# First token tile's gate product moved into the output banks, ahead of the second tile's dt product and running sums

## The chip, the core and the metric

The kernel runs on one core of one Trainium2 chip. The metric is device time in microseconds of one execution of the program. Timed runs of the kernel before gave 942.22 to 943.0, median 942.59.

## The reference

One layer on 256 tokens of width 512, all in fp32: a cross-attention to 4096 context rows, a Mamba-2 block, and a mixture of 32 experts, each added to the residual x. The change lies in the Mamba block, which with its projections and its scan is:

```python
zxbcdt = einsum("bld,ed->ble", u, W_in)          # u: layernorm of x
z, xBC, dt = split(zxbcdt)                       # 1024, 1280, 16 columns
xBC = silu(causal_conv1d(xBC, conv_w, conv_b))   # 4 taps, per channel
dt = softplus(dt + dt_bias); dA = dt * -exp(A_log)
A_cs = cumsum(dA)                                # within a chunk of 128 tokens
Lmat = tril(exp(A_cs[l] - A_cs[s]))
Y = C B^T * Lmat @ (x dt)  +  C @ state * exp(A_cs)  +  x D
y = rmsnorm(Y * silu(z)) * norm_weight
out = y @ W_out
```

## The kernel before, in words

The 256 tokens are two tiles of 128; each tile is one chunk of the scan, and only tile 1 receives a carried state. The whole layer is one program. Attention over the context fills the first 720 us; tile 0's share of the Mamba block up to its decays is run beside the last attention steps. Then come the output projection of attention for tile 1, the rest of the Mamba block, the routing, and the experts.

**Who sets the order.** The Python text calls small closures. A scheduler then gives every engine one fixed order, from the order of the text, the dependencies, the tile buffers and its own estimate of durations; so an instruction can stand earlier or later than its line. `tc.issue_after(x)` keeps what is issued under it behind instruction x in that order. On the chip each engine works through its own list and waits on semaphores.

**PSUM.** There are eight banks. Six are in a ring that `bank(name)` hands out in turn (pools `ps_mm`, `ps_sc`, `ps_tp`); the two others are `ps_o`, tag "o", in which `within(t)` makes a tile's output, `ps_yd`.

The steps of the Mamba block that matter here, with their names and the lines of the kernel before:

- `product()` of tile t: `turn_xn` transposes the layernorm's result on TensorE into a bank (`lnT`, L227) and copies it to `xT` in two halves, one on VectorE and one on ScalarE (L231). Then `project` (L237) makes the dt product `ps_dt`: four matmuls of 16 columns. VectorE adds the bias (L984) and ScalarE takes an exponential (L987).
- `series()`: some fifteen VectorE instructions on 128x16 values, softplus by a series, which end in `dA` (L1000).
- `sums()`: the running sums `ps_cs` (L1005), a matmul of `dA` with a triangle of ones, copied to `acs` (L1008).
- `decays(t)`: its first step, `spread_sums` (`lm[0]`), makes the sums transposed (`ps_csT`, L1023), copies them (L1024), writes them to DRAM by a DMA from ScalarE's queue (L1025), and reads them back from GpSimd's queue, broadcast to all partitions, into `lm` (L1026) and, for tile 1, into `e1` (L1030). Its four pieces subtract `acs` on VectorE (L1034, 16 instructions) and take the exponential on ScalarE (L1038); the last also takes that of `e1` (L1040).
- `channels(t)`: ten pieces, one for every 128 channels of xBC. Four matmuls (`ps_xbc`, L237), two ScalarE instructions (L1054, L1055), then three taps of the convolution, on VectorE (L1063), or for the channel tiles 3 and 7 on ScalarE and GpSimd (L1060, L1061). `active()` is one Silu over all ten (L1066), called as `silu[t]()`.
- `gates(t)`: for each half j of 512 columns of z, 16 matmuls of 128 columns (`ps_z`, L237) with the weights `w_z[j]`, and a Silu into `zs` (L1078).
- `assemble(t)`: `y` from `ps_yd` (L1153), times the gate (L1154), its square (L1155), times the norm's weight (L1156), and the sums of the squares (L1158).
- `tokens_back(t)`: eight transposes of the activated channels (`xtT`, L1088) and a product with dt (L1090).
- `mixing(t)`: `ps_g` (L1098) and its product with the decays, on VectorE and GpSimd (L1102).
- `carried(t)`, `within(t)`, `mamba_out(t)`: `ps_off` (L1136), `ps_yd` (L1110), and the output projection `ps_out` (L1163).
- `hold(...)`: gives buffers that are no longer needed to the experts' weights, and starts the loads on SyncE's queue (L1406); the first of them wait for the start of tile 1's decays.

The list `order` is the channel tiles 8, 9, 0, 1 ... 7: B and C first.

Of the kernel before, what the change touches and what calls it, by code (L numbers as in the profile page):

```python
# [11 lines left out]
FP = mybir.dt.float32  # L12
U32 = mybir.dt.uint32
I32 = mybir.dt.int32
AF = mybir.ActivationFunctionType
# [4 lines left out]
P = 128  # L20
# [9 lines left out]
REP = NH // NKV  # L30
# [10 lines left out]
SH = 16  # L41
# [3 lines left out]
CONV = 4  # L45
# [39 lines left out]
def perceiver_layer(ctx: ExitStack, tc: tile.TileContext, a: dict, out: bass.AP):  # L85
    nc = tc.nc
    V, S, G, TE = nc.vector, nc.scalar, nc.gpsimd, nc.tensor
# [62 lines left out]
    def layer(ctx, bounded):  # L150
# [10 lines left out]
        xT = keep.tile([P, KD, L], FP, name="xT")  # L161
# [62 lines left out]
        def turn_xn(t, tp, halves=False):  # L224

            for k in range(KD):
                TE.transpose(tp[:, k * P:(k + 1) * P], xn[:, t, k * P:(k + 1) * P], ident)  # L227

            for copy, ks in (((V.tensor_copy, slice(0, KD // 2)), (S.copy, slice(KD // 2, KD))) if halves else
                             ((V.tensor_copy, slice(0, KD)),)):  # L230
                turned = copy(xT[:, ks, t * P:(t + 1) * P], tp.rearrange("p (k n) -> p k n", k=KD)[:, ks])  # L231
            return turned

        def project(ps, lhs, rhs_of):

            for k in range(KD):
                last = TE.matmul(ps, lhs(k), rhs_of(k), start=(k == 0), stop=(k == KD - 1))  # L237
            return last

        conv_w, conv_b, norm_w, d_col = carve(by_channel, (XCT, CONV), (XCT,), (DIT,), (DIT,))  # L240
# [420 lines left out]
        q = [[lambda j=j, t=t: q_of(j, t) for t in range(NT)] for j in range(4)]  # L661
# [262 lines left out]
        ps_o = pool("ps_oT", 2, space=PSUM) if bounded else None  # L924
        m = {}
        banks = ring([(ps_mm, "mm")])

        def bank(name):
            p, tag = banks()
            return p.tile([P, 512], FP, tag=tag, name=name)  # L930
# [30 lines left out]
        tok = lambda t: slice(t * P, (t + 1) * P)  # L961
# [13 lines left out]
        def steps_of(t):  # L975


            vdt, nab, u, z, z2, ser, dt, dA, acs = (m[n, t] for n in ("vdt", "nab", "u", "z", "z2", "ser", "dt", "dA", "acs"))

            def product():  # L980
                turn_xn(t, bank("lnT"), halves=True)
                ps = bank("ps_dt")
                project(ps[:, 0:SH], lambda k: xT[:, k, tok(t)], lambda k: m["w_bcd"][:, k, 256:272])
                V.tensor_tensor(vdt, ps[:, 0:SH], dt_bias, ALU.add)  # L984
                V.tensor_scalar(nab, vdt, -1.0, None, ALU.mult)
                V.tensor_tensor(nab, nab, vdt, ALU.min)
                S.activation(u, nab, AF.Exp)  # L987

            def series():
                V.tensor_scalar(z, u, 2.0, None, ALU.add)  # L990
                V.reciprocal(z, z)
                V.tensor_tensor(z, z, u, ALU.mult)
                V.tensor_tensor(z2, z, z, ALU.mult)
                V.tensor_scalar(ser, z2, 1.0 / 15.0, None, ALU.mult)
                for d in (13, 11, 9, 7, 5, 3):
                    V.scalar_tensor_tensor(ser, ser, 1.0 / d, z2, ALU.add, ALU.mult)
                V.scalar_tensor_tensor(ser, ser, 1.0, z, ALU.add, ALU.mult)
                V.tensor_scalar(vdt, vdt, 0.0, None, ALU.max)
                V.scalar_tensor_tensor(dt, ser, 2.0, vdt, ALU.mult, ALU.add)
                V.scalar_tensor_tensor(dA, dt, -1.0, m["ea", 0], ALU.mult, ALU.mult)  # L1000

            def sums():

                ps = bank("ps_cs")
                TE.matmul(ps[:, 0:SH], upper, dA, start=True, stop=True)  # L1005
                if t == 0:
                    TE.matmul(ps[:, SH:2 * SH], ones, dA, start=True, stop=True)
                V.tensor_copy(acs, ps[:, 0:SH])  # L1008
                if t == 0:
                    V.tensor_tensor(m["decay", 0], ps[:, SH:2 * SH], acs, ALU.subtract)  # L1010
                    S.activation(m["decay", 0], m["decay", 0], AF.Exp)
            return product, series, sums

        decay_begun = []

        def decays(t):


            lm, acs = m["lm"], m["acs", t]

            def spread_sums():
                ps = bank("ps_csT")[0:SH, 0:P]
                TE.matmul(ps, m["dA", t], upper, start=True, stop=True)  # L1023
                S.copy(m["csT", t], ps)  # L1024
                S.dma_start(sums_d[t], m["csT", t])  # L1025
                G.dma_start(lm, sums_d[t].partition_broadcast(P))  # L1026
                if t > 0:
                    pairs = sums_d[t].rearrange("(c e) l -> e c l", e=2)
                    for i in range(2):
                        G.dma_start(m["e1"][lanes(i)], pairs[i].partition_broadcast(SP))  # L1030

            def piece(q):
                for hh in range(q * 4, q * 4 + 4):
                    begun = V.tensor_scalar(lm[:, hh, :], lm[:, hh, :], acs[:, hh:hh + 1], 0.0, ALU.subtract, ALU.min)  # L1034
                    if hh == 0:
                        decay_begun.append(begun)
                with tc.issue_after(gated[-1]) if gated else nullcontext():
                    S.activation(lm[:, q * 4:q * 4 + 4, :], lm[:, q * 4:q * 4 + 4, :], AF.Exp)  # L1038
                    if t > 0 and q == 3:
                        S.activation(m["e1"], m["e1"], AF.Exp)  # L1040
            return [spread_sums] + [lambda q=q: piece(q) for q in range(4)]

        def channels(t):


            xc, xraw = m["xc", t], m["xraw"]

            def piece(ct):
                w, c0 = ((w_x[ct // 4], ct % 4 * P) if ct < 8 else (m["w_bcd"], (ct - 8) * P))
                ps = bank("ps_xbc")[:, 0:P]  # L1050
                project(ps, lambda k: w[:, k, c0:c0 + P], lambda k: xT[:, k, tok(t)])
                xb = xraw[:, ct, :]
                y = xc[:, ct, :]
                S.copy(xb[:, CONV - 1:], ps)  # L1054
                S.activation(y, ps, AF.Identity, bias=conv_b[:, ct:ct + 1], scale=conv_w[:, ct, CONV - 1:CONV])  # L1055
                for j in range(CONV - 1):
                    w = conv_w[:, ct, j:j + 1]
                    if ct % 4 == 3:
                        tap = small.tile([P, P], FP, tag="tap", name="tap", bufs=2)
                        S.activation(tap, xb[:, j:j + P], AF.Copy, scale=w)  # L1060
                        G.tensor_tensor(y, y, tap, ALU.add)  # L1061
                    else:
                        V.scalar_tensor_tensor(y, xb[:, j:j + P], w, y, ALU.mult, ALU.add)  # L1063

            def active():
                S.activation(xc, xc, AF.Silu)  # L1066
                if t + 1 < NT:
                    G.tensor_copy(xraw[:, :, 0:CONV - 1], xraw[:, :, P:P + CONV - 1])
            return [lambda ct=ct: piece(ct) for ct in range(XCT)], active

        gated = []

        def gates(t):
            def piece(j):
                ps = bank("ps_z")
                for i in range(4):
                    project(ps[:, tok(i)], lambda k: w_z[j][:, k, tok(i)], lambda k: xT[:, k, tok(t)])
                gated.append(S.activation(m["zs"][:, t, j * 512:(j + 1) * 512], ps, AF.Silu).ins)  # L1078
            return [lambda j=j: piece(j) for j in range(2)]

        def tokens_back(t):

# [345 lines left out]
        run = lambda fs: [f() for f in fs]  # L1428
        order = [XCT - 2, XCT - 1] + list(range(XCT - 2))
# [18 lines left out]
        else:  # L1448
            general_attention()
            ps_o = pool("ps_oT", 2, space=PSUM)  # L1450
# [5 lines left out]
        product, series, sums = steps_of(1)  # L1456
        chans, silu = zip(*(channels(t) for t in range(NT)))
# [8 lines left out]
        w_z = [wpiece(a["W_inT"][:, c0:c0 + 512], f"w_in{c0}") for c0 in (0, 512)]  # L1466
# [7 lines left out]
        run(within(0))  # L1474
        state()
        routing_memory()
        product()
        series()
        lm = decays(1)
        run(chans[1][c] for c in order[0:3])  # L1480
        sums()
        lm[0]()
        run(chans[1][c] for c in order[3:])
        run(gates(0))
        run(lm[1:])

        hold(*w_x, lacc[:, 0], behind=decay_begun[-1])
# [1 line left out]
        silu[1]()  # L1489
        run(tokens_back(1))  # L1490
        mixing(1)()
        run(gates(1))
        hold(*w_z)
        run(carried(1))
        run(within(1))
# [19 lines left out]
        product, gate0, turn0 = shared_hidden(0)  # L1515
# [9 lines left out]
        product, gate1, turn1 = shared_hidden(1)  # L1525
# [184 lines left out]
        with ExitStack() as rctx:  # L1710
# [42 lines left out]
            copied = main.turn(0)  # L1753
# [103 lines left out]
    with tc.If(flag == 1) as arms:  # L1857
        with ExitStack() as lctx:
            layer(lctx, True)
# [51 lines left out]
```

## Time and profile before

| what | value |
|---|---|
| median of 3 runs | 942.59 us (942.22 to 943.0) |
| the profiled execution's own time | 946.23 us |
| its span, first to last instruction | 944.3 us |
| mean granted TensorE clock | 0.997 |
| PE busy | 924.2 us, 98% |
| weight loads on PE | 504.9 us, 53% |
| VectorE, ScalarE, GpSimd busy | 577.4, 370.0, 427.8 us |
| chain that ended last | PE 96%, VectorE 2% |
| all gate products, ps_z, in that chain | 1% of the span |

Times in the profile count from the span's start. PE is TensorE's matmuls, PEld its weight loads, DVE VectorE, ACT ScalarE, POOL GpSimd, SP SyncE. L12 is line 12 of the kernel. An fp32 matmul leaves two records. A line of the timeline gives the start, the duration, engine, line and operation, what it writes and reads, and in brackets the idle time before it with the instruction that ended it. The chain that ended last is followed back from the last instruction, at each step to what released it. PEclk is the clock that TensorE was granted, 1.00 at full speed.

### The profile page before, as it was taken

The numbers are of one execution on the slowest core, as the hardware profiler recorded it, in microseconds if no ns is written. First come the engines' busy times: TensorE is split into PE (matmuls) and PEld (weight loads), VectorE is DVE, ScalarE is ACT, GpSimd is POOL, SyncE is SP. The second block draws the span as 40 slices with busy tenths as digits, with TensorE's granted clock in tenths as the row PEclk, the third lists the DMA queues.
The fourth block names the chain that finished last, engine by engine and source line by source line (L and its number), as shares of the span: only waits on it lengthen the run. The fifth ranks groups of instructions, "written<-read, shape, count | busy, mean of one in ns | idle before, by whom it ended". The sixth has DMA issues, their size and how long they took to land.

```text
span 944.3 us, 10567 instructions
## 1 busy us (share of the span) xinstructions
PE 924.2 (98%) x3266; PEld 504.9 (53%) x3266; DVE 577.4 (61%) x1199; ACT 370.0 (39%) x853; POOL 427.8 (45%) x498
## 2 busy tenths in 40 slices
PE   7999999999999999999999999999999999999996
PEld 3444555555555555555555555554465775654332
DVE  4866766566666665756666656658588685661224
ACT  4556444344344343443444434434154442022121
POOL 3769846345544644724725544220013251545542
PEclk9999999999999999999999999999999999999999
DMA  9651053053024114204305203090025481779983
GB/s 331 203 112 58 1 179 89 1 154 92 1 66 146 33 31 159 57 3 154 90 0 157 68 1 89 14 298 1 0 101 197 145 309 68 288 287 348 421 330 101
DMA packets 129716, 122.33 MB, mean 130 GB/s; under 512 B 79889, under 2 KB 99122, under 8 KB 124402
## 3 DMA queue, kind: packets, MB, share of 16 engines
q1 hardware_dynamic: 118960, 77.43, 27.2%
q0 software_dynamic: 7504, 39.59, 11.3%
q10 hardware_dynamic: 3186, 4.54, 1.3%
q8 instruction: 28, 0.46, 0.2%
q14 instruction: 38, 0.31, 0.1%
HBM read 89.54 MB, written 32.00 MB: 129 GB/s over the span
## 4 chain that ended last, share of the span: by engine, by line
PE 96%; DVE 2%; DMA 0%; issue 0%; ACT 0%; POOL 0%; SPq 0%; ACTq 0%
PE oT L774 24%; PE scT L748 24%; PE ps_kv L522 16%; PE ps_self L237 4%; PE ps_egu L1629 3%; PE ps_o L969 3%; PE ps_egu L237 3%; PE ps_first L399 3%; PE ps_xbc L237 2%; PE ps_out L1163 1%; PE ps_z L237 1%; PE xgTp L1601 1%; PE ps_ye L1651 1%; PE ps_ye L1652 1%; PE total L1670 1%; PE ps_ye L1700 1%
## 5 line engine op out<-in xcount | busy, mean ns | idle before, releaser
L765 DVE TENSOR_TENSOR lacc<-lacc,prT 128x512 f32<-128x512 f32 x256 | 199.8, 781 | 198.0 <-ACT prT L754 196.6
L754 ACT ACTIVATE prT<-scT,bq,rk 128x512 f32<-128x512 f32 x256 | 198.4, 775 | 280.9 <-PE scT L748 268.8
L748 PE MATMUL scT<-qT,kT 128*128 128x512 f32 x536 | 273.5, 592 | 0.0
L774 PE MATMUL oT<-prT,v 128*128 128x512 f32 x528 | 269.4, 592 | 0.0
L774 PEld LDWEIGHTS oT<-prT,v 128*128 128x128 f32 x528 | 100.2, 190 | 125.3 <-issue 118.6
L748 PEld LDWEIGHTS scT<-qT,kT 128*128 128x128 f32 x536 | 101.3, 190 | 41.4 <-issue 30.8
L522 PE MATMUL ps_kv<-fast,ctx 128*128 128x256 f32 x350 | 99.5, 379 | 0.0
L522 PEld LDWEIGHTS ps_kv<-fast,ctx 128*128 128x128 f32 x350 | 66.5, 190 | 47.9 <-issue 39.9
L471 POOL TENSOR_TENSOR ctx<-ctx 128x128 f32<-128x128 f32 x21 | 10.4, 495 | 98.7 <-PE ps_kv L522 98.7
L211 POOL TENSOR_TENSOR rk<-pv,mhalf 128x4 f32<-128x4 f32 x32 | 38.7, 1219 | 27.3 <-DVE pv L210 27.1
L522 PE MATMUL ps_kv<-wkv,ctx 128*128 128x256 f32 x168 | 48.8, 379 | 0.0
L282 ACT ACTIVATE xn<-kraw 128x128 f32<-128x128 f32 x112 | 33.5, 301 | 38.5 <-POOL kraw L497 21.5
L507 POOL TENSOR_TENSOR v<-fast,v 128x768 f32<-128x768 f32 x21 | 40.8, 1958 | 16.5 <-DVE fast L551 15.9
L522 PEld LDWEIGHTS ps_kv<-wkv,ctx 128*128 128x128 f32 x168 | 31.9, 190 | 28.2 <-issue 24.6
L780 DVE TENSOR_TENSOR oacc<-oT,oacc 128x512 f32<-128x512 f32 x64 | 43.7, 682 | 0.0
L1394 POOL DMA_INDIRECT xg_sb<-xd,listed x21 | 20.1, 959 | 31.7 <-DVE lacc L1258 14.4
L522 PE MATMUL ps_kv<-fast,fast 128*128 128x256 f32 x112 | 33.3, 379 | 0.0
L1633 DVE TENSOR_TENSOR hid<-si,ps_egu 128x128 f32<-128x128 f32 x11 | 3.2, 288 | 47.0 <-ACT si L1631 40.0
L522 PEld LDWEIGHTS ps_kv<-fast,fast 128*128 128x128 f32 x112 | 21.3, 190 | 17.8 <-issue 12.0
L288 DVE STREAM_TRANSPOSE tr<-kraw 128x512 f32<-128x512 f32 x28 | 18.3, 690 | 19.6 <-POOL kraw L496 19.6
L469 POOL TENSOR_TENSOR ctx<-fast 128x128 f32<-128x128 f32 x28 | 20.4, 730 | 19.6 <-PE ps_kv L522 19.1
L969 PE MATMUL ps_o<-wo,qT 128*128 128x512 f32 x64 | 28.8, 592 | 0.0
(423 smaller groups left out, 1399.9 us busy)
## 6 DMA issues: line engine op xcount, KB each, us to landing
xg<-xn SPq DMA_DIRECT2D x6, 2560.0 KB
ctx<-in_ctxT_dram SPq DMA_DIRECT2D x7, 1024.0 KB, 4.7
kd<-tr SPq DMA_DIRECT2D x112, 64.0 KB, 2.2
kT<-kd SPq DMA_DIRECT2D x28, 256.0 KB, 2.8
wq<-in_wq_dram SPq DMA_DIRECT2D x4, 1024.0 KB, 10.4
wo<-in_wo_dram SPq DMA_DIRECT2D x4, 1024.0 KB
w_in<-in_W_inT_dram SPq DMA_DIRECT2D x4, 1024.0 KB, 11.7
w_in<-in_experts_dram SPq DMA_DIRECT2D x4, 1024.0 KB, 6.9
```

The lines of the kernel that those rows point to most:

```text
L211: return G.tensor_tensor(dst, v[:, :n], mhalf[:, :n], ALU.pow)
L237: last = TE.matmul(ps, lhs(k), rhs_of(k), start=(k == 0), stop=(k == KD - 1))
L282: S.activation(sq[:, h, :], raw[:, h, :], AF.Square, accum_out=ss[:, h:h + 1])
L399: TE.matmul(ps, lhs[:, j, k, :], rhs[:, k, :], start=(start and k == 0), stop=(k == 1), skip_group_check=True)
L507: G.tensor_tensor(to[:, 1:4], q, base[:, 1:4], ALU.add)
L522: TE.matmul(b[n], sets[name][i], y, start=start, stop=True, skip_group_check=True)
L748: scored.append(TE.matmul(sc, kT[:, g, i * P:(i + 1) * P], qT[:, t, heads4(g), :].rearrange("p h q -> p (h q)"), start=True, stop=True).ins)
L754: S.activation(pr, sc, AF.Exp, bias=shift, scale=SCALE if r is None else r[:, i, g:g + 1])
L765: V.tensor_tensor(la, la, pr, ALU.add)
L774: TE.matmul(outs[g, t], v[:, i, g * HD:(g + 1) * HD], pr, start=(n == 0), stop=last)
L780: V.tensor_tensor(ov, outs.pop((g, t)), ov, ALU.add)
L969: TE.matmul(m["ps_o", t], aT[:, t, h, :], wo[j][:, h % 4, :], start=(h == 0), stop=(h == NH - 1))
```

## The change

`gates(t)` is taken apart: its pieces now make the matmuls of some of the four column blocks alone and return a context that holds what is issued in it behind them; the Silu is a function of its own, `opened`, held behind a given instruction. Tile 0's gate goes to the two `ps_o` banks instead of two of the ring. Two of the four blocks of its first half are issued ahead of tile 1's dt product, the other two and the whole second half after seven channel tiles and ahead of tile 1's running sums. Seven channel tiles of tile 1 instead of three precede the sums in the text, and three instead of seven follow. The Silus of tile 0's gate are held behind the last channel's first reading, those of tile 1's behind the last exponential of the decays.

```diff
-            def product():
+            def product(between=nullcontext):
                 turn_xn(t, bank("lnT"), halves=True)
                 ps = bank("ps_dt")
-                project(ps[:, 0:SH], lambda k: xT[:, k, tok(t)], lambda k: m["w_bcd"][:, k, 256:272])
+                with between():
+                    project(ps[:, 0:SH], lambda k: xT[:, k, tok(t)], lambda k: m["w_bcd"][:, k, 256:272])
...
-                    S.activation(lm[:, q * 4:q * 4 + 4, :], lm[:, q * 4:q * 4 + 4, :], AF.Exp)
+                    m["decayed"] = S.activation(lm[:, q * 4:q * 4 + 4, :], lm[:, q * 4:q * 4 + 4, :], AF.Exp).ins
...
-                S.activation(y, ps, AF.Identity, bias=conv_b[:, ct:ct + 1], scale=conv_w[:, ct, CONV - 1:CONV])
+                m["copied"] = S.activation(y, ps, AF.Identity, bias=conv_b[:, ct:ct + 1], scale=conv_w[:, ct, CONV - 1:CONV]).ins
...
         def gates(t):
-            def piece(j):
-                ps = bank("ps_z")
-                for i in range(4):
-                    project(ps[:, tok(i)], lambda k: w_z[j][:, k, tok(i)], lambda k: xT[:, k, tok(t)])
-                gated.append(S.activation(m["zs"][:, t, j * 512:(j + 1) * 512], ps, AF.Silu).ins)
-            return [lambda j=j: piece(j) for j in range(2)]
+            def piece(j, columns=range(4)):
+                if columns[0] == 0:
+                    m["ps_z", t, j] = bank("ps_z") if t > 0 else ps_o.tile([P, REP * P], FP, tag="o", name="ps_z")
+                ps = m["ps_z", t, j]
+                for i in columns:
+                    last = project(ps[:, tok(i)], lambda k: w_z[j][:, k, tok(i)], lambda k: xT[:, k, tok(t)])
+                return tc.issue_after(last.ins)
+            def opened(j, behind):
+                with tc.issue_after(behind):
+                    gated.append(S.activation(m["zs"][:, t, j * 512:(j + 1) * 512], m["ps_z", t, j], AF.Silu).ins)
+            return [lambda *columns, j=j: piece(j, *columns) for j in range(2)], opened
...
-        product()
+        (gate0, gate1), opened = gates(0)
+        product(lambda: gate0(range(2)))
         series()
         lm = decays(1)
-        run(chans[1][c] for c in order[0:3])
-        sums()
+        run(chans[1][c] for c in order[0:7])
+        gate0(range(2, 4))
+        with gate1():
+            sums()
         lm[0]()
-        run(chans[1][c] for c in order[3:])
-        run(gates(0))
+        run(chans[1][c] for c in order[7:])
+        for j in range(2):
+            opened(j, m["copied"])
         run(lm[1:])
...
         mixing(1)()
-        run(gates(1))
+        products, opened = gates(1)
+        for j in range(2):
+            products[j]()
+            opened(j, m["decayed"])
         hold(*w_z)
```

## The prediction

> **What bounds the kernel now.** I read the page's chain that ended last first: 96% of it is PE. So only what opens or closes a gap on PE counts, and I looked for the gaps around the change in PE's waits from 700 us on (line, who was waited for, us in total, times, longest):
>
> ```profile
> PE ps_z L237 <- ACT xc L1055: 0.7, 1, 0.7
> PE ps_cs L1005 <- DVE xc L1000: 0.6, 1, 0.6
> PE ps_dt L237 <- DVE xT L231: 0.5, 1, 0.5
> ```
>
> These three are all that independent matmuls could fill here: 0.52 us before the dt product, 0.71 before a gate product that lacks a bank, 0.59 before the running sums, 1.82 in all. Next the timeline of PE (start, us, engine, line, records):
>
> ```profile
> 736.95 0.66 PE L227 MATMUL lnT<-ident,xn 128*128 128x128 f32 x4 [0.24 <-DVE xn L221]
> ...
> 745.63 0.40 PE L1005 MATMUL ps_cs<-xc,upper 128*128 128x16 f32 x2 [0.59 <-DVE xc L1000]
> 745.95 0.39 PE L1023 MATMUL ps_csT<-upper,xc 128*16 128x128 f32 x2
> 746.28 5.62 PE L237 MATMUL ps_xbc<-xT,w_in 128*128 128x128 f32 x48
> 751.74 6.19 PE L237 MATMUL ps_z<-xT,w_in 128*128 128x128 f32 x54
> 757.77 1.04 PE L1088 MATMUL xtT<-ident,xc 128*128 128x128 f32 x8
> ...
> 758.86 7.31 PE L237 MATMUL ps_z<-xT,w_in 128*128 128x128 f32 x64
> ```
>
> The reader should see that the transpose of the sums (ps_csT) leaves PE at 746.28, and that xtT, which turns tile 1's activated channels xc back, comes 11.5 us later. An fp32 product shows as two records. Then ACT and DVE in the same stretch:
>
> ```profile
> 756.00 1.26 ACT L1066 ACTIVATE xc<-xc 128x1280 f32<-128x1280 f32 x1
> 757.97 0.60 ACT L1078 ACTIVATE wkv<-ps_z 128x512 f32<-128x512 f32 x1 [0.70 <-PE ps_z L237]
> 758.58 1.28 ACT L1038 ACT_TABLE_LOAD   x1
> 759.88 2.19 ACT L1038 ACTIVATE lm<-lm 128x512 f32<-128x512 f32 x4
> 761.97 1.04 ACT L1040 ACTIVATE wkv<-wkv 128x1024 f32<-128x1024 f32 x1
> ```
>
> ```profile
> 753.78 3.50 DVE L1034 TENSOR_SCALAR lm<-lm,xc 128x128 f32<-128x128 f32 x16 [0.25 <-DMA lm<-sums]
> ```
>
> xc's Silu (L1066) stands ahead of the decays' exponentials (L1038, L1040), and ends at 757.26, before PE reaches xtT. The decays wait for lm, which comes back through DRAM: from the end of ps_csT to L1034 it takes 753.78 - 746.28 = 7.5 us.
>
> **What the change does to each engine's order.** Each engine has one fixed order, and the changed program's can be read without running it. PE:
>
> ```
> lnT, ps_z(tile 0) x8, ps_dt x4, ps_xbc 7 channel tiles, ps_z(tile 0) x24, ps_cs, ps_csT,
> ps_xbc 3 channel tiles, ps_z(tile 1) x16, xtT, ps_g, ps_z(tile 1) x16, ps_off, ps_yd, ps_out
> ```
>
> ACT, behind the copies of the last three channel tiles:
>
> ```
> table load, Silu gate 0, Silu gate 1, 2 squares, table load (waits for lm's DMA), Exp lm q0, tap,
> Exp lm q1 q2 q3, Exp e1, table load, Silu xc, Silu gates of tile 1
> ```
>
> So two things move that the edit does not name. ps_csT goes behind 24 more products. And xc's Silu, on which xtT waits, goes behind the exponentials, which wait for that very round trip. No instruction's work is added: the products, activations and table loads are as many as before. The two output banks (tag o) are free, since L1153 has read them by 735.6, before lnT; their next users, ps_yd of tile 1, come after the Silus. The bank ring loses two takes, and no bank is the late one in what follows.
>
> **The sum, PE.** lnT takes 4 x 0.117 from 736.95, next issue 737.42. Eight ps_z products: 16 records x 0.1117 (64 records in 7.15 in the chain) = 1.79, 739.21. ps_dt: 0.47 + 0.37, as its two halves took before, 740.05; that is some 0.6 later for the series on DVE, which is covered, since the sums are now not asked for before 751. Seven channel tiles: 56 x 0.1138 (48 in 5.46) = 6.37, 746.42. 24 products: 48 x 0.1117 = 5.36, 751.78. ps_cs and ps_csT 0.65, 752.43. Three channel tiles 2.73, 755.16. Sixteen products 3.57: PE is at xtT at **758.7**. All three gaps are filled.
>
> **The sum, ACT.** ps_csT ends 752.43 - 746.28 = 6.15 later, so lm lands at 753.75 + 6.15 = 759.9. The last channel copy follows PE by 0.20 as before, 755.35; identity and two taps end 1.20 later, 756.55; the table load takes 1.30, so the gates' Silus start at 757.85 and 758.34. DVE multiplies them in (L1154 twice, L1156: 0.68, 0.60 and 0.67 back to back) until 760.4, and ACT has squared both by then. Now the Exp table load, 760.4 to 761.7; L1034's 16 take 3.50, to 763.9, and the four exponentials follow them; the last ends at 764.5. e1 adds 1.0, the Silu table 1.30, xc's Silu 1.26: **768.05**. PE stands still from 758.7, 9.3 us.
>
> **The sum, back to the chain.** Behind xtT PE has xtT 0.87, ps_g 0.22, sixteen products 3.57, ps_off 1.79, ps_yd 1.90 = 8.35, so ps_out starts at 776.4 instead of 769.86: **+6.5 us**. That already contains the gaps filled. lm is not late behind it: POOL's two products L1102 (3.47) start once L1148 (2 x 1.03) and gu are done, about 770.9, and end near 774.4, when ps_yd begins. From ps_out to the end the chain is PE with its old dependencies, so the shift stays. The expert loads on SP shift too (first at 754.13 before, about 759 to 762 after); their first reader ran at 810.04, so that is covered.
>
> **The clock.** A gap of 9.3 us has no like in the trace; the longest PE wait from 700 us on is 2.1 and left the clock alone. But after PE's last matmul ends at 937.89 the clock falls, and it has fallen once under light work (columns: window, span, busy of PE, PEld, DVE, ACT, POOL, then PEclk):
>
> ```profile
> 940.00:941.00 1.00, 0.00 (x0) 0.00 (x0) 0.00 (x0) 0.00 (x0) 0.00 (x0) 1.00 0.34 92
> 941.00:942.00 1.00, 0.00 (x0) 0.00 (x0) 0.00 (x0) 0.00 (x0) 0.00 (x0) 0.70 0.08 27
> 942.00:943.00 1.00, 0.00 (x0) 0.00 (x0) 0.00 (x0) 0.00 (x0) 0.00 (x0) 0.50 0.09 25
> ```
>
> 0.70 over 941 to 942 is a fall to a half at 941.4, 3.5 us into the idle time. So I expect PE to come back at half clock. What that costs is read where it happened at work: 0.76, 0.50, 0.50 and 0.54 in the four windows from 818 to 822, 1.70 us of clock lost, and eight ps_egu records took 3.84 against 2.74. Bounds 0 to 1.7; I take 1.7, because the gap is more than twice 3.5 us and everything behind xtT is bound by PE. Together **+8.2 us**.
>
> The Trainium skill, in "TensorE: Matmul & The Clock Gate", "Why this matters for your kernels", asks for no PE-idle gaps over about 3 us between bursts of matmuls; this speaks against the change as built, and the row above agrees with it.
>
> On the table loads a page and the trace differ. In the trace the load takes 1.28 and the next activation starts 1.30 after its start (758.58 to 759.88). I use 1.30. "ScalarE: Activation LUTs", "What ACT_TABLE_LOAD costs", counts 2.66 us for each switch, a drain included; by it the three loads in this chain would make the sum up to 4.1 us more.
>
> **Bounds.** Below: no clock loss and 0.8 of error in the ACT chain, +5.7. Above: L1154 and L1156 at the slower 1.53 and 1.42 seen beside POOL before (+1.6), and up to 0.6 of lateness of lm, since SP's load into w_z[0] now starts at about 758.8, ahead of those into w_x, while lm is landing: +10.4.
>
> **Rivals.** (1) PE is not held, and the fill is kept: the three gaps go, 942.6 - 1.8 = 940.8, or up to 942.6 if lm is then late at ps_yd. For it: the waits are there, and ps_z fits them. Against it: xc's Silu would have to end by 758.7, 9.3 us earlier than I find, behind an Exp load that itself waits for lm at 759.9. That is the point from which it decides. 0.08, of which 0.03 below 940.7. (2) The hold without the clock: 942.6 + 6.5 = 949.1. For it: no idle time between matmuls lost the clock so far, and the drop at 818 came with PE at work. 0.17. (3) The hold, longer: the slower DVE rows and a late lm, 942.6 + 10 = 952.6. For it: L1154 ran at 1.53 here once; against: POOL, beside which it did, waits for xc in the changed order. 0.13. My forecast keeps 0.62.
>
> **The numbers.** The profiled execution took 946.23 (span 944.3), 3.64 above the median 942.59 of the runs; the shift is added to the median: 942.59 + 8.2 = 950.8. In a profile it would be a span of about 952.5. The range takes the bounds, +5.7 to +10.4, so 948.3 to 953.0, which covers all but rival 1 and tails. About 0.2% (1.9 us) is what a measurement of this kernel can tell from no change: faster by more than that 0.03, within it 0.05, slower 0.92.
>
> **What would show it.** Right: xtT waits 8 to 11 us for ACT xc; L1034 starts some 6 to 7 us later; xc's Silu stands behind e1's Exp; the waits of ps_dt, ps_z and ps_cs are gone; the clock is below 1 just behind the gap. Wrong: xtT starts within 1 us of 758.7, or the same gap is made up in ps_out or later, or lm's landing does not move with ps_csT.

## The result and the profile after

The changed kernel took 953.96 us (median; 951.97 to 957.0) where the kernel before took 942.8 (942.22 to 943.6): ratio 1.0102 [1.0062, 1.0142]. Measured again on another chip it was 950.51 against 939.83, ratio 1.0113 [1.0099, 1.0128]. (The ratios are estimates with a 95% interval and not quotients of the medians; that quotient would be 1.0118 here.) The shift is thus 9.6 us by the first ratio, 11.2 between the first medians and 10.7 on the second chip; the prediction had +8.2, with bounds of +5.7 and +10.4. The median of 953.96 lies 1.0 above the upper end of the forecast range, 953.0; 942.59 times the ratio is 952.2, inside it. The profiled execution took 957.0 (span 955.0, mean clock 0.989).

The helper code grew by a few lines, so L1034, L1066, L1088, L1163 of before are L1035, L1067, L1094, L1169 here. PE's waits from 700 us on in the changed kernel (line, who was waited for, us in total, times, longest):

```profile
PE xtT L1094 <- ACT xc L1067: 11.2, 1, 11.2
...
PE lnT L227 <- DVE xn L221: 0.2, 1, 0.2
```

The waits of ps_dt, ps_z and ps_cs (1.82 us in all) are gone, and one wait of 11.2 us stands in their place. PE's timeline in the changed kernel:

```profile
736.54 0.66 PE L227 MATMUL lnT<-ident,xn 128*128 128x128 f32 x4 [0.25 <-DVE xn L221]
737.03 1.95 PE L237 MATMUL ps_z<-xT,w_in 128*128 128x128 f32 x16
738.82 0.96 PE L237 MATMUL ps_dt<-w_bcd,xT 128*128 128x16 f32 x8
...
745.96 5.52 PE L237 MATMUL ps_z<-xT,w_in 128*128 128x128 f32 x48
751.32 0.29 PE L1006 MATMUL ps_cs<-xc,upper 128*128 128x16 f32 x2
751.55 0.39 PE L1024 MATMUL ps_csT<-upper,xc 128*16 128x128 f32 x2
...
754.65 3.74 PE L237 MATMUL ps_z<-xT,w_in 128*128 128x128 f32 x32
769.58 1.97 PE L1094 MATMUL xtT<-ident,xc 128*128 128x128 f32 x8 [11.19 <-ACT xc L1067]
...
771.76 4.91 PE L237 MATMUL ps_z<-xT,w_in 128*128 128x128 f32 x32
```

From lnT to the arrival at xtT PE never waits: 758.39. Thirty-two gate records take 3.74 us ahead of the wait and 4.91 behind it, and xtT takes 1.97 where it took 1.04: PE came back at a lower clock. ACT in the same stretch:

```profile
756.07 1.28 ACT L1084 ACT_TABLE_LOAD   x1
757.37 1.09 ACT L1084 ACTIVATE wkv<-ps_z 128x512 f32<-128x512 f32 x2
758.72 1.23 ACT L1161 ACTIVATE ctx<-qT 128x512 f32<-128x512 f32 x2 [0.27 <-DVE qT L1160]
761.84 1.28 ACT L1039 ACT_TABLE_LOAD   x1 [1.89 <-DMA lm<-sums]
...
765.90 1.04 ACT L1041 ACTIVATE wkv<-wkv 128x1024 f32<-128x1024 f32 x1
766.96 1.28 ACT L1067 ACT_TABLE_LOAD   x1
768.25 1.27 ACT L1067 ACTIVATE xc<-xc 128x1280 f32<-128x1280 f32 x1
```

The reader should see ACT with nothing to do for 1.89 us, held by the load of the Exp table that itself waits for lm, while xc's Silu stands behind that load, four exponentials, the one of the tile `e1` and a second table load. VectorE shows the same landing:

```profile
761.80 3.53 DVE L1035 TENSOR_SCALAR lm<-lm,xc 128x128 f32<-128x128 f32 x16 [1.91 <-DMA lm<-sums]
```

That is 8.0 us later than the 753.78 of before; ps_csT itself moved by 5.6 (745.95 to 751.55). Last the clock (window, span, busy of PE, PEld, DVE, ACT, POOL, then PEclk, DMA share, GB/s):

```profile
759.00:760.00 1.00, 0.00 (x0) 0.00 (x0) 0.89 (x2) 0.95 (x2) 0.00 (x0) 1.00 1.08 270
760.00:761.00 1.00, 0.00 (x0) 0.00 (x0) 0.00 (x0) 0.00 (x0) 0.00 (x0) 0.79 1.07 184
761.00:762.00 1.00, 0.00 (x0) 0.00 (x0) 0.20 (x1) 0.16 (x1) 0.00 (x0) 0.50 0.98 238
...
773.00:774.00 1.00, 1.00 (x7) 1.00 (x6) 1.00 (x1) 0.00 (x0) 1.00 (x2) 0.50 0.02 8
774.00:775.00 1.00, 1.00 (x10) 1.00 (x10) 1.00 (x2) 0.00 (x0) 1.00 (x1) 0.89 0.00 0
```

The clock fell to a half at 760.6, 2.2 us into the gap, and stayed there until about 774.2 (0.89 in the last window), 4.6 us after PE had work again.

To compare runs whose profiled executions differ elsewhere in the program, I use one stretch of PE's timeline: from tile 1's lnT (736.54 here) to the next lnT, that of tile 0 inside tile 1's `mamba_out` (790.99 here). It was 43.59 us before (736.95 to 780.54) and is 54.45 now: +10.86, nearly the whole difference.

### The profile page after: what moved, and what is told of

It reads as the page before. It is cut to its first block, busy times and chain, and to the rows that moved or that the text cites. A ratio compares the mean times of both kernels' runs of the same rounds, so it can differ in the third digit from the quotient of the medians.

```text
span 955.0 us, 10565 instructions
## 1 busy us (share of the span) xinstructions
PE 925.4 (97%) x3266; PEld 507.0 (53%) x3266; DVE 575.4 (60%) x1199; ACT 370.0 (39%) x853; POOL 425.1 (45%) x498
## 3 DMA queue, kind: packets, MB, share of 16 engines
q0 software_dynamic: 7504, 39.59, 11.2%
## 4 chain that ended last, share of the span: by engine, by line
PE 95%; DVE 2%; DMA 1%; issue 1%; ACT 1%; POOL 0%; SPq 0%; ACTq 0%
PE oT L774 24%; PE scT L748 24%; PE ps_kv L522 16%; PE ps_self L237 4%; PE ps_egu L1642 3%; PE ps_o L969 3%; PE ps_egu L237 3%; PE ps_first L399 3%; PE ps_xbc L237 2%; PE ps_out L1169 1%; PE ps_z L237 1%; PE xgTp L1614 1%; PE ps_ye L1664 1%; PE ps_ye L1665 1%; PE total L1683 1%; PE ps_ye L1713 1%
## 5 line engine op out<-in xcount | busy, mean ns | idle before, releaser
L471 POOL TENSOR_TENSOR ctx<-ctx 128x128 f32<-128x128 f32 x21 | 10.4, 495 | 98.6 <-PE ps_kv L522 98.6
L211 POOL TENSOR_TENSOR rk<-pv,mhalf 128x4 f32<-128x4 f32 x32 | 38.2, 1203 | 27.3 <-DVE pv L210 27.1
```

What stands on the lines that cost most here:

```text
L211: return G.tensor_tensor(dst, v[:, :n], mhalf[:, :n], ALU.pow)
```

## The experiments

Theory A: the loss is the place of xc's Silu in ACT's order, behind exponentials that wait for lm's trip through DRAM; the late sums and the cold clock make it longer. Theory B: the late sums are enough by themselves, since the decays are needed at ps_yd whatever ACT does first. A third question was what the three filled gaps are worth once the wait is gone.

The ratio of each experiment is against the kernel before on its own chip (942.73 us for e1 to e4, 940.32 for e5 to e8, 939.83 for e9 to e12). The stretch comes from the one profiled execution of each run and is against the 43.59 us of the only profile of before, which was taken on the first chip:

| kernel | time us | ratio | stretch against before | wait at xtT |
|---|---|---|---|---|
| changed (second chip: e9) | 950.51 | 1.0113 [1.0099, 1.0128] | +9.78 | 10.8 |
| e7 late Silu alone, PE as before | 952.7 | 1.0122 [1.0106, 1.0137] | +11.23 | 8.8 |
| e1 Silu first | 947.71 | 1.0044 [1.0018, 1.007] | +5.08 | 3.8 |
| e2 sums first | 951.05 | 1.0079 [1.0052, 1.0106] | +7.29 | 8.5 |
| e3 both | 943.04 | 0.999 [0.9965, 1.0014] | +0.43 | 1.9 |
| e4 both, Silu ahead of the gates' | 943.54 | 1.0006 [0.9979, 1.0033] | +1.37 | 1.0 |
| e5 load later | 951.38 | 1.0117 [1.0102, 1.0133] | +10.67 | 10.3 |
| e6 warm | 949.02 | 1.009 [1.0076, 1.0104] | +8.69 | 1.4 |
| e8 warm, load later | 948.43 | 1.0089 [1.0075, 1.0103] | +7.62 | 0.3 |
| e10 the first quarter only | 946.32 | 1.0061 [1.0048, 1.0074] | +5.57 | 5.2 |
| e11 the quarter, Silu first | 942.0 | 1.0018 [1.0009, 1.0027] | +0.55 | none |
| e12 Silu first, load later | 945.1 | 1.005 [1.0037, 1.0062] | +5.46 | 3.8 |

**e7, the Silu alone.** The kernel before, with one edit: xc's Silu is held behind the last exponential of the decays.

```diff
-                    S.activation(lm[:, q * 4:q * 4 + 4, :], lm[:, q * 4:q * 4 + 4, :], AF.Exp)
+                    m["decayed"] = S.activation(lm[:, q * 4:q * 4 + 4, :], lm[:, q * 4:q * 4 + 4, :], AF.Exp).ins
                     if t > 0 and q == 3:
-                        S.activation(m["e1"], m["e1"], AF.Exp)
+                        m["decayed"] = S.activation(m["e1"], m["e1"], AF.Exp).ins
...
-        silu[1]()
+        with tc.issue_after(m["decayed"]):
+            silu[1]()
```

> The kernel before, with nothing moved on TensorE, and only the Silu of tile 1's channels held behind the decays' exponentials on ScalarE. Theory A: lm lands at 753.8 as before, the exponentials end near 762, e1, squares and a table load follow, the Silu ends near 766.5; xtT, which stands at 757.8 there, waits about 8.5 us, half a gate more of products lies behind it, and the clock halves: 951 to 956. Theory B (late sums): no loss, 942 to 943.

Measured: ratio 1.0122 [1.0106, 1.0137], as large a loss as the change's. PE's waits:

```profile
PE xtT L1088 <- ACT xc L1066: 8.8, 1, 8.8
PE ps_z L237 <- ACT xc L1055: 0.7, 1, 0.7
PE ps_cs L1005 <- DVE xc L1000: 0.6, 1, 0.6
PE ps_dt L237 <- DVE xT L231: 0.5, 1, 0.5
```

Not a matmul has moved, all three old gaps are there, and the long wait appears, with the clock (64 gate records behind it take 8.57 instead of 7.31). So the place of the Silu is sufficient for the loss. It is not the only way to lose, as the next runs show.

**e1, the Silu first.** The changed kernel with xc's Silu ahead of the exponentials; PE's order stays.

```diff
             def active():
-                S.activation(xc, xc, AF.Silu)
+                m["active", t] = S.activation(xc, xc, AF.Silu).ins
...
         for j in range(2):
             opened(j, m["copied"])
+        silu[1]()
+        gated.append(m["active", 1])
         run(lm[1:])
...
-        silu[1]()
```

> The changed kernel with one thing turned round: the Silu of tile 1's channels is held ahead of the decays' exponentials on ScalarE; TensorE's order stays as changed. Theory A (the Silu's place is what holds TensorE): the Silu then ends near 761.5, xtT waits about 3 us instead of 11, the clock stays near 1, and ps_out starts near 770: 942 to 945 us. Theory B (the late running sums are what holds it, through the decays, wherever the Silu stands): the wait moves to ps_yd and the time stays at 949 or more.

Measured: 1.0044, between the two expectations. The waits:

```profile
PE xtT L1094 <- ACT xc L1067: 3.8, 1, 3.8
PE ps_yd L1116 <- POOL lm L1108: 0.8, 2, 0.6
```

```profile
762.61 1.97 PE L1094 MATMUL xtT<-ident,xc 128*128 128x128 f32 x8 [3.82 <-ACT xc L1067]
...
764.80 5.14 PE L237 MATMUL ps_z<-xT,w_in 128*128 128x128 f32 x32
```

More than half of the loss is gone. Three things are left. One is a wait for the Silu, which now starts at 761.28 behind POOL's last tap. That tap needs one on ACT, which stands at 760.26, behind the gates' Silus and the squares, so this wait too is ACT's order and not the late sums. The second is a clock at a half from about 761 until 767.7: from xtT to ps_out it takes 12.06 us (762.61 to 774.67), 0.83 of which are waits at ps_yd, where e6 below needs 8.50 at full clock. That is 2.7 us, no less than behind the longer gap of the change (2.2). The third is 0.8 us at ps_yd, where the decays are now late: B's mechanism, at a smaller size than A's.

**e2, the sums first.** The sums and `lm[0]` ahead of the second to fourth quarters of the gate; the Silu stays late.

```diff
         run(chans[1][c] for c in order[0:7])
+        sums()
+        lm[0]()
         gate0(range(2, 4))
-        with gate1():
-            sums()
-        lm[0]()
+        gate1()
```

> The changed kernel with the running sums and their transpose ahead of the 24 gate products instead of behind them; ScalarE's order keeps the Silu of the channels behind the exponentials. Theory A: lm lands near 754, but the gates' Silus, the exponentials, e1 and a table load still stand ahead of the Silu; xtT starts near 766.6, waits about 8 us and the clock still halves: 949 to 951. Theory B: with the sums early the loss is gone: 941 to 943.

Measured: 1.0079, and lm is first used at 755.16 instead of 761.80. If the late sums alone made the loss, it should have gone; but PE still waits 8.5 us at xtT for the Silu. It starts there at 766.60, just where expected.

```profile
PE xtT L1094 <- ACT xc L1067: 8.5, 1, 8.5
```

**e3 and e4, both.** e3 makes the edits of e1 and e2 together. e4 also puts xc's Silu ahead of the two Silus of the gate:

```diff
...
+        silu[1]()
         for j in range(2):
-            opened(j, m["copied"])
+            opened(j, m["active", 1])
...
-        silu[1]()
```

> Both turned round: sums ahead of the 24 gate products, Silu of the channels ahead of the exponentials (behind the gates' Silus). Theory A: the Silu ends near 760.2, xtT waits about 1.5 us, the three small gaps stay filled: 941 to 942.5. If the output banks or the eight products ahead of the dt product cost something by themselves: 943.5 or more.

> As the run before, and the Silu of the channels stands ahead of the gates' Silus too, directly behind the last taps. Theory A: it ends near 758.7, where TensorE arrives at xtT; all three gaps of before are filled and nothing opens in their place: 940.5 to 941.6. If the decays are then late at ps_yd: 942 or more, with the wait at ps_yd.

Measured: e3 0.999 and e4 1.0006, both intervals around 1. The loss is cured. The gain of the filled gaps does not show: the intervals, some 0.25% to each side, would hide 1.8 us, but the stretches are no shorter than before (+0.43 and +1.37). In e3 PE waits 1.9 us at xtT and 0.97 more at tile 0's lnT inside `mamba_out`. The gap of 1.9 us leaves the clock alone, xtT taking 1.09 behind it:

```profile
760.37 1.09 PE L1094 MATMUL xtT<-ident,xc 128*128 128x128 f32 x8 [1.90 <-ACT xc L1067]
```

In e4 the wait at xtT is 1.0, and:

```profile
PE ps_yd L1116 <- POOL lm L1108: 1.5, 2, 1.0
PE lnT L227 <- DVE xn L221: 1.2, 2, 1.0
```

What is saved at one wait is met again at the next.

**e10, the first quarter only.** Only the first two gate blocks fill the gap at ps_dt; the order of channels and sums is that of before, and the rest of the gate follows the channels.

```diff
-        run(chans[1][c] for c in order[0:7])
-        gate0(range(2, 4))
-        with gate1():
-            sums()
+        run(chans[1][c] for c in order[0:3])
+        sums()
         lm[0]()
-        run(chans[1][c] for c in order[7:])
+        run(chans[1][c] for c in order[3:])
+        gate0(range(2, 4))
+        gate1()
```

> The first half of the change alone: a quarter of tile 0's gate ahead of the dt product and the output banks, while the running sums stay behind three channel tiles as before and the rest of the gate follows the channels. ScalarE's order still has the Silu of the channels behind the exponentials. Theory A (the Silu's place decides): xtT starts near 766 to 767, waits 7 to 8 us, the clock halves: 0.8 to 1.1% slower than before, although the sums are early. Theory B (late sums decide): no slower than before.

Measured: 1.0061, a smaller loss than expected, in A's direction. lm is early, yet the Silu is still behind the exponentials:

```profile
PE xtT L1094 <- ACT xc L1067: 5.2, 1, 5.2
PE ps_cs L1006 <- DVE xc L1001: 0.6, 1, 0.6
```

The wait is shorter than in e2 because the Exps (757.61) and so the Silu (763.09) come some 2.2 us earlier, and because PE comes to xtT 1.1 us later (759.23 against 758.13).

**e11, the quarter with the Silu first.** e10, with the Silus in the order half 0 of the gate, xc, half 1 of the gate, all ahead of the exponentials.

```diff
...
-        for j in range(2):
-            opened(j, m["copied"])
+        opened(0, m["copied"])
+        silu[1]()
+        opened(1, m["active", 1])
...
-        silu[1]()
```

> The run before with the Silu of the channels held between the two Silus of tile 0's gate, as it stood in the kernel before. Theory A: nothing holds xtT, lm is as early as before, and the three small gaps stay filled: 1.0 to 1.8 us faster than before (0.1 to 0.2%), the wait at xtT under 1 us. If the gaps are given back at ps_yd or later: the same as before.

Measured: 1.0018 [1.0009, 1.0027], slower by 1.7 to 2.2 us, not faster; a miss, and the most instructive of them. PE has no wait at xtT (757.62), two of the three gaps are gone, and ps_out starts 31.10 us behind lnT instead of 32.84: 1.7 us are really saved there. Then PE meets this, in its timeline:

```profile
780.95 0.63 PE L227 MATMUL lnT<-ident,xn 128*128 128x128 f32 x4 [2.25 <-DVE xn L221]
```

To see why xn is no earlier, DVE and POOL of e11 behind the decays:

```profile
763.32 2.37 DVE L1108 TENSOR_TENSOR lm<-lm,gu 128x512 f32<-128x512 f32 x2
765.61 2.54 DVE L1164 TENSOR_TENSOR ctx<-ctx 128x512 f32<-128x512 f32 x3
768.07 1.28 DVE L1144 TENSOR_TENSOR off<-ps_off,wkv 128x512 f32<-128x512 f32 x2
...
780.26 0.55 DVE L221 TENSOR_SCALAR xn<-x_sb,mv,rs 128x512 f32<-128x512 f32 x1 [0.66 <-POOL rs L211]
```

```profile
768.90 2.49 POOL L1156 TENSOR_TENSOR qT<-qT,off 128x512 f32<-128x512 f32 x2 [2.08 <-DVE off L1144]
774.57 2.59 POOL L1164 TENSOR_TENSOR ctx<-ctx 128x512 f32<-128x512 f32 x3 [3.18 <-ACT ctx L1161]
777.12 0.56 POOL L211 TENSOR_TENSOR ry<-pv,mhalf 128x1 f32<-128x1 f32 x1
```

DVE has no idle time from 754.21, when lm lands, to 769.35 (decays, gate, norm, ctx, lm, squares, `off`). `off` stands last there, so it starts at 768.07 although PE is done with ps_off by 766.1, and POOL waits for it. POOL's sums of squares (L1164) stand ahead of its small step L211, from which the layernorm and its xn follow. The same rows in the kernel before are at 762.89, 765.19, 767.65 on DVE, 768.48 and 774.15 on POOL: 0.42 earlier, although PE is at ps_out 1.9 us later; lm lands 0.43 earlier there (753.78). So this chain is paced by lm's landing and DVE's work behind it, and not by PE. In e11 xn ends at 780.26 + 0.55 = 780.81 and PE, which waits for it, starts 0.14 later. In the kernel before:

```profile
779.85 0.55 DVE L221 TENSOR_SCALAR xn<-x_sb,mv,rs 128x512 f32<-128x512 f32 x1 [0.66 <-POOL rs L211]
```

```profile
775.18 5.40 PE L1163 MATMUL ps_out<-w_out,qT 128*128 128x512 f32 x12
780.54 0.63 PE L227 MATMUL lnT<-ident,xn 128*128 128x128 f32 x4
```

There xn ends at 779.85 + 0.55 = 780.40, and lnT starts at 780.54, the same 0.14 later, just as PE is done with ps_out: xn was only just in time, and an earlier PE would have waited for it. The stretch of e11 is +0.55, and its profiled execution took 940.36 us, 0.53 more than the median of before. The median of its runs is another 1.6 higher; where those executions lose it stays open.

**e6 and e8, a warm clock.** Forty-four matmuls into an unused bank keep PE at work ahead of xtT; they add work and change no result. e8 also defers the load of e5.

```diff
...
+        with products[0]():
+            spare = bank("spare")
+            for i in range(44):
+                last = TE.matmul(spare[:, 0:P], w_z[1][:, i % KD, 0:P], xT[:, i % KD, tok(1)], start=True, stop=True)
+        with tc.issue_after(last.ins):
+            run(tokens_back(1))
+            mixing(1)()
...
```

> The changed kernel with 44 matmuls of 128 columns, whose result nobody reads, put on TensorE between the first half of tile 1's gate and xtT: some 9.8 us of work added into the gap. Theory A (the clock falls in the gap and is paid for afterwards): the wait at xtT shrinks to about 1 us, the clock stays at 1, and the kernel with more work is about 2 us faster than the changed one: 950.5 to 952.5. If the clock costs nothing here: the same as the changed kernel, 953 to 955.

> The idle matmuls and the later load together. If the two extra costs are separate and add up: about 4 us less than the changed kernel, 948.5 to 950.5, which leaves the 6.5 us of the hold itself. If they are the same thing: no less than the better of the two alone.

Measured: 1.009 and 1.0089, against 1.0117 for e5 on the same chip, whose clock falls. PE's timeline in e6:

```profile
757.59 9.99 PE L1504 MATMUL spare<-xT,w_in 128*128 128x128 f32 x88
768.97 1.09 PE L1094 MATMUL xtT<-ident,xc 128*128 128x128 f32 x8 [1.39 <-ACT xc L1067]
...
770.12 3.74 PE L237 MATMUL ps_z<-xT,w_in 128*128 128x128 f32 x32
```

xtT starts no earlier, but it and the gate records run at full speed, and with more work the kernel is faster than e5 by 2.4 us (e6) and 3.0 us (e8, which differs from e5 only in the matmuls and in what is held behind them). From xtT to ps_out it takes 8.50 us here (768.97 to 777.47), 10.71 in the first profile of the change, 10.06 in its second (e9), 11.42 in e5: the lower clock costs 2.2, 1.6 and 2.9 us. e8 was expected 4 us below the changed kernel if the two costs added up; it is 3.0 below e5 and 0.6 below e6, so they do not.

**e5 and e12, the load into w_z.** The prediction named this load on SP's queue as a possible reason for a late lm. e5 is the changed kernel, e12 is e1, each with it held behind the decays' start.

```diff
-        hold(*w_z)
+        hold(*w_z, behind=decay_begun[-1])
```

> The changed kernel, but the first expert load into w_z[0], which SP starts at 758.4 while lm is on its way, waits for the start of tile 1's decays like the loads into w_x. Theory A (that load takes DMA time from lm): lm lands some 2 us sooner, near 759.8, everything behind follows: about 2 us less than the changed kernel, 950 to 952. If lm is late for another reason: no change, 953 to 955.

> Late sums as in the changed kernel, but the Silu of the channels ahead of the exponentials and the load into w_z[0] behind the start of the decays. Theory A: with the Silu off the decays' path the wait at xtT is about 3.5 us and what is left is lm's lateness at ps_yd; the later load gives about 1 us of that back: 0.2 to 0.4% slower than before.

Measured: e5 1.0117 against 1.0113 of the change itself, e12 1.005 against 1.0044 of e1: no gain, though both comparisons cross chips; e8 against e6, on one chip, is 1.0089 against 1.009. A miss in time. The profiles say more. lm's first use in e6 and in e8:

```profile
761.19 3.53 DVE L1035 TENSOR_SCALAR lm<-lm,xc 128x128 f32<-128x128 f32 x16 [1.94 <-DMA lm<-sums]
```

```profile
760.69 3.52 DVE L1035 TENSOR_SCALAR lm<-lm,xc 128x128 f32<-128x128 f32 x16 [0.88 <-DMA lm<-sums]
```

Counted from the copy of csT (751.34 and 751.89), that is 9.85 us with the load in its old place and 8.80 with the load later; in e5 it is 8.93, against 9.82 and 9.40 in the two profiles of the change. But in e12, where the load starts only at 762.18, lm is still read first 9.92 us behind the copy (751.91 to 761.83), against 9.52 in e1. So the load may cost about 1 us of the trip in the changed kernel. It is not all that makes lm late, and in e12 holding it back saved nothing.

**e9, the change again,** as the reference of the last four runs:

> The changed kernel once more, unaltered, so that it stands beside the three others and the kernel before on one chip. The hold of 9 to 11 us at xtT and 2 us of clock: 1.1 to 1.3% slower than before; lm lands 9 to 10 us after ps_csT.

It behaves as expected: 1.13% slower, lm's first use 9.4 us behind the copy of csT. Its gap is 10.8 us; its clock falls later (0.72 in the window 762 to 763) and recovers sooner (0.67 in 772 to 773) than in the first profile.

## Why the prediction was right in sign and mechanism, and short in size

- **PE's order and arrival: right.** 758.7 was predicted with lnT at 736.95; measured 758.39 with lnT at 736.54, which agrees to 0.1. All three gaps were filled.
- **The cause: right.** xc's Silu behind the exponentials, these behind lm. e7 shows that this alone makes a loss as large, e1 (and e12 against e9 on one chip, 1.005 and 1.0113) that taking it away removes more than half, e2 that early sums alone leave most of it; e3, with both, is back at 1.
- **lm's landing: the term that was mis-sized.** The sum moved lm by as much as ps_csT, to 759.9, and let the table load start at 760.4, when ACT is free. The trip from the copy of csT to the first use of lm was 7.40 us before (746.38 to 753.78) and 9.82 here (751.98 to 761.80). The sign that was given, a start of L1034 some 6 to 7 us later, was missed: it is 8.0. Against a PE 0.41 ahead that puts the table load 1.9 later than in the sum. From there on the sum holds: load to start of the Silu is 6.41 us (761.84 to 768.25), predicted 760.4 to 766.79, 6.39. So two table loads at 1.30 fit; the 2.66 us that the Trainium skill counts for each ("ScalarE: Activation LUTs", "What ACT_TABLE_LOAD costs") would have made it 9.1. I had taken at most 0.6 for such lateness, and for one reason, the load into w_z: e8 and e5 allow it up to about 1 us, e12 none, and the rest of the 2.4 us has another cause.
- **The clock: right that it falls, a little small.** 1.7 was taken from the windows at 818; 2.2 us here, 1.6 in e9 and 2.9 in e5. The half clock came 2.2 us into the gap, not 3.5. The Trainium skill's rule against gaps of over about 3 us ("TensorE: Matmul & The Clock Gate", "Why this matters for your kernels") pointed the right way: the gap of 3.8 us in e1 halved the clock, the one of 1.9 us in e3 did not.
- **The sum.** +8.2, with 1.9 for lm, 0.5 for the clock and 0.15 for the work behind xtT, gives +10.7; the stretch shows +10.86. The 0.15 is an error of the sum: from xtT to ps_out it had 8.35, where e6 takes 8.50 at full clock; it counted ps_off at 1.79, where the rows of before give 1.88 (766.01 to 767.89).
- **Rivals.** (1) did not happen, and its price was wrong as well: with PE hardly held the gaps give nothing (stretch +0.43 in e3, +1.37 in e4, +0.55 in e11; the time of e11, 1.0018 [1.0009, 1.0027], excludes a gain), not 1.8 us. The rows for it, xn's end on DVE just ahead of PE's second lnT, were in the trace of before, behind the point at which I stopped following the chain ("from ps_out to the end the chain is PE with its old dependencies"). (2), no clock loss, is refuted by the clock rows above and by e6 and e8. (3) came about in its second half only: lm late. Its first half did not: L1160 ran at 0.65 each here (two in 1.29), not 1.53.

What stays open is why lm's trip is longer. Of the change's 9.82 us, 7.62 lie between POOL's issue of the read (754.18) and the first use, where it was 5.19 before (748.59 to 753.78): the extra 2.4 us lies between the issue of the read and its landing. Trips that began near 746 to 748 took 7.1 to 8.0 us (before, e2, e3, e4, e7, e10, e11), those that began near 752 took 8.8 to 9.9 (both profiles of the change, e1, e5, e6, e8, e12). No run separates the read from what it shares the queue with, the two reads of the tile `e1` that POOL issues right behind, or from POOL's taps, which follow these issues at once in the changed kernel (756.24) and only at 752.94, 2.3 us behind them, in the kernel before.

No run beat the kernel before by more than its interval.

## What to carry to other kernels

Before independent matmuls are moved into TensorE's gaps, compare every engine's order, not only TensorE's: an activation that falls behind one that waits for a DRAM round trip cost far more here (10.7 us) than the gaps (1.8). Then follow the chain past the filled gaps to the next place where another engine joins, and read how much slack it has; here the chain on VectorE behind lm left none, so the 1.8 us of gaps could not become time. In these runs a gap of 3.8 us (e1) or more on TensorE cost its own length and 1.4 (e2) to 2.9 us (e5) more at half clock behind it.

## What the runs showed of the hardware

- The clock's fall and recovery have no fixed delay in these rows: the half came 2.2 us into the gap in the first profile of the change and 3.8 us in the second (e9; PE idle from about 758.6), and it lasted through 4.6 and 3.3 us of work behind it. Over the other runs the fall lies between 2.1 (e1) and 4.5 us (e2, 0.81 in the window 762 to 763), and the work at half clock between 2.8 (e2) and 6.1 us (e5). The gap of 1.9 us in e3 brought no fall. Unused matmuls in the gap kept it at 1.00 and made the kernel faster than e5 by 2.4 to 3.0 us.
- One broadcast read of 1 MB with two of 256 KB behind it on GpSimd's queue was first used 4.9 us (e10) to 7.7 us (e12) after its issue. With SyncE's load held back it was 6.7 (e5), 6.6 (e8) and 7.7 (e12), without that 7.2 to 7.7 in the same late place (the change, e9, e1, e6).
